# Cross attention in a decoder layer: the distance bias added by TensorE, maxima and exponentials taken for four tiles at once

## The chip, the core and the metric

The kernel runs on one core of a Trainium2 chip. The core has five engines that work side by side and each through its own list of instructions: TensorE (PE) multiplies matrices and writes its results to PSUM, VectorE (DVE) does elementwise work and reductions, ScalarE (ACT) does exponentials, other functions and copies, GpSimd (POOL) helps, and SyncE (SP) starts transfers. They wait for one another by semaphores. The metric is device time in microseconds (us). All data are fp32.

## The reference

One post-norm decoder layer for 4 batches of 1024 tokens of width 256: self attention with two further attentions nested in it, cross attention to 154 context tokens, and a mixture of experts. Each of the three parts is added to its input and normalised. The change concerns the cross attention, which has 16 heads of width 16:

```python
q = (query @ Wq.T + bq) * d ** (-0.5)
k = key_ @ Wk.T + bk
v = value @ Wv.T + bv
...
scores = jnp.einsum('bhqd,bhkd->bhqk', q, k)
distance_bias = -jnp.log(distances + 1e-09) * jnp.abs(distance_scaling)
scores = scores + distance_bias[:, None, :, :]
attn = jax.nn.softmax(scores, axis=-1)
out = jnp.einsum('bhqk,bhkd->bhqd', attn, v)
```

The bias depends on the batch, the query token and the context token, but not on the head: every head adds the same 1024 x 154 numbers.

## The kernel before, in words

The program goes through the batches one after the other and, at the end, through the experts for all of them. In a batch come the self attention, two attentions with four heads, a projection with a normalisation (close_sublayer), the cross attention, and a second such closing.

The cross attention first makes the keys kx, the values vx and the bias tile. The bias tile has the 128 tokens of a tile on its partitions and, for each of the 8 token tiles, 154 context tokens in a row; ACT takes the logarithm (line 942) and DVE the scaling (line 943). Then the loop of lines 951 to 961 runs over 32 units. Unit n belongs to a group g of four heads, a pair of token tiles tp, and a pair of heads in the group:

- scores(n), lines 654 to 689: four products on PE (line 662), one for each of 2 token tiles x 2 heads. Each takes 32 rows of q and of kx, so it uses 32 rows of PE's array; the two heads lie in different rows. The results, 4 x 154 columns, go to one PSUM tile called big, of which there are two for the whole kernel; each head has a bank of it. The helper biased (line 267) then lets DVE do a fused operation for each of the four: it adds bias, negates, stores the sum to the tile xs in SBUF and leaves its minimum in a column of xmx. ACT takes the exponential of each of the four with that column as its bias (line 682).
- flip(n), lines 691 to 706, two rounds later: eight transposes on PE (line 697) into two PSUM tiles called one, of which there are three, and copies back to SBUF, by ACT, or by DVE for the second half of odd units.
- product(n), lines 708 to 725, after each second unit: eight products on PE (line 716, sixteen records) weigh the values, a copy on ACT (line 724), and two rounds later, by the due times of the class Clock, divide (lines 351 to 355) transposes the result on PE and divides it by the row sums on DVE.

The softmax's sums come from a column of ones in the values, so nothing else is taken from the exponentials. The queries of the next four heads are projected at each eighth unit (lines 647 to 652 and 955), and the first ones before the loop.

In the first three batches the loop also takes one step a round of begin(b + 1), the generator that starts the next batch's self attention (maxima, which use big too, and value projections). In the last batch there is nothing to take. The framework orders each engine's instructions when the program is built, near program order, but it may draw work of this kind into a wait: in the first three batches PE does value projections (line 302) between the query projection and the first scores.

Of the kernel before, what the change touches and what calls it, by code (L numbers as in the profile page):

```python
# [8 lines left out]
F32 = mybir.dt.float32  # L9
I32 = mybir.dt.int32  # L10
U32 = mybir.dt.uint32
AF = mybir.ActivationFunctionType
ALU = mybir.AluOpType
AX = mybir.AxisListType
PSUM = bass.MemoryType.PSUM

P = 128
B, S, H = 4, 1024, 256
S2 = 154
# [27 lines left out]
def decoder_layer(ctx: ExitStack, tc: tile.TileContext, a, out):  # L47
    nc = tc.nc
# [8 lines left out]
    def big():  # L57
        return pbig.tile([P, 2, 512], F32, tag="big", name="big")

    def small():  # L60
        return pone.tile([P, 512], F32, tag="one", name="one")
# [18 lines left out]
    ident = const.tile([P, P], F32, name="ident")  # L80
# [52 lines left out]
    with tc.tile_pool(name="wA", bufs=1) as wA, tc.tile_pool(name="work", bufs=2) as work:  # L133
# [76 lines left out]
        ps = small()  # L210
# [53 lines left out]
        def ex_tile(shape, name):  # L264
            return work.tile(shape, F32, tag="ex", name=name, bufs=EXB)

        def biased(out, ps, bias, low):

            nc.vector.tensor_tensor_reduce(  # L269
                out=out,  # L270
                in0=ps,
                in1=bias,
                scale=-1.0,
                scalar=3.0e38,
                op0=ALU.add,
                op1=ALU.min,
                accum_out=low,
            )
# [239 lines left out]
        def mha_units(qk, v, weight, cx):  # L518
# [93 lines left out]
            for u in range(n + 2):  # L612
                pss = scores(u) if u < n else None
                if 1 <= u <= n:
                    flip(u - 1, 0)
                if u < n:
                    exponentials(u, pss)
                if 1 <= u <= n:
                    flip(u - 1, 1)
                    del probs[u - 1]  # L620
                if u >= 2:
                    product(u - 2)
                yield

        def out_features(w, cx, c):

            ps = big()
            for tb in range(2):
                for pair in range(2):
                    nc.tensor.matmul(  # L630
                        ps[:, tb, :],
                        w[4][:, pair, c * P : (c + 1) * P],
                        cx[:, pair, tb * 512 : (tb + 1) * 512],
                        start=(pair == 0),
                        stop=(pair == 1),
                    )
            return ps


        class Cross:  # L640
# [13 lines left out]
            def scores(self, n):  # L654
                g, s = divmod(n, 8)
                tp, pair = divmod(s, 2)
                ps = big()
                for tt in range(2):
                    for jj in range(2):
                        r = 32 * (2 * pair + jj)  # L660
                        tok = (2 * tp + tt) * P
                        nc.tensor.matmul(  # L662
                            ps[:, jj, tt * S2 : (tt + 1) * S2],
                            self.q[g][r : r + 32, tok : tok + P],
                            self.kx[r : r + 32, g, :],
                            start=True,
                            stop=True,
                        )
                ex = ex_tile([P, 2, 2, S2], "xs")
                mx = work.tile([P, 4], F32, tag="xmx", name="xmx", bufs=3)  # L670
                for tt in range(2):
                    for jj in range(2):
                        biased(
                            ex[:, jj, tt, :],
                            ps[:, jj, tt * S2 : (tt + 1) * S2],
                            self.bias[:, 2 * tp + tt, :],
                            mx[:, 2 * tt + jj : 2 * tt + jj + 1],
                        )
                for tt in range(2):
                    for jj in range(2):  # L680
                        i = 2 * tt + jj
                        nc.scalar.activation(  # L682
                            ex[:, jj, tt, :],
                            ex[:, jj, tt, :],
                            AF.Exp,
                            bias=mx[:, i : i + 1],
                            scale=-1.0,
                        )
                self.ex[n] = ex

            def flip(self, n):
# [120 lines left out]
        for b in range(B):  # L812
            y = ys[b]

            bias = work.tile([P, NT, S2], F32, tag="bias", name="bias", bufs=1)
# [39 lines left out]
            for c in range(NC2):  # L855
                ps = out_features(ca, cx2, c)
# [23 lines left out]
            for c in range(NC2):  # L880
                ps = out_features(mc, cx3, c)
# [14 lines left out]
            ps = big()  # L896
# [9 lines left out]
            ps = big()  # L906
            for g in range(NG):
                for c in range(NC2):
# [4 lines left out]
                        start=(c == 0),  # L913
                        stop=(c == NC2 - 1),
                    )
            for g in range(NG):
# [4 lines left out]
                    bias=xbk[:, g : g + 1],  # L921
# [3 lines left out]
            for k in range(2):  # L925
                ps = small()
                for c in range(NC2):
# [4 lines left out]
                        start=(c == 0),  # L932
                        stop=(c == NC2 - 1),
# [117 lines left out]
    ps = small()  # L1051
# [287 lines left out]
```

## Time and profile before

| what | value |
|---|---|
| median of 3 runs | 3434.65 us (3431.64 to 3437.42) |
| the profiled execution's own time | 3433.82 us |
| its span, first to last instruction | 3432.0 us |
| mean granted clock of TensorE | 0.976 |
| stretch 632 to 760 us, the first cross attention: PE / DVE / ACT busy | 125.09 / 75.75 / 80.96 of 128 us |
| stretch 2668 to 2776 us, the last one: PE / DVE / ACT busy | 101.24 / 63.37 / 75.01 of 108 us |
| flips of the cross attention, PE line 697 | 1024 records, mean 283 ns |
| scores of the cross attention, PE line 662 | 1024 records, mean 324 ns |

PE is the engine of matrix products, PEld its weight loads. A record's duration runs from its start to its modelled end, and records overlap: the share of time that PE advances is read from the distance between records, or from the chain of work that ended last, not from their mean. An fp32 product makes two records, a transpose one. The granted clock is 1.00 when TensorE gets its full clock.

### The profile page before, as it was taken

Reading aid. Unit: us, or ns where it says so; the run is one execution under the profiler, and the core shown is the slowest. Engines: PE = TensorE matmul, PEld = TensorE weight load, DVE = VectorE, ACT = ScalarE, POOL = GpSimd, SP = SyncE. Lnnn points to the kernel's source line nnn. Section 1 sums busy time; section 2 is a strip of 40 time slices with the busy share of each in tenths; the row PEclk is TensorE's granted clock in tenths of the full one; section 3 lists DMA queues with packets and bytes.
Section 4 is the critical chain, followed back from the end, with each engine's and each line's share of the span. In section 5 each row is a group of like instructions: output and inputs, shape, how many; then the busy total and the mean of one; then the engine's idle time right before and its main releaser. Section 6 shows DMA issues by size and latency. Waiting matters only on the chain.

```text
span 3432.0 us, 60936 instructions
## 1 busy us (share of the span) xinstructions
PE 3300.5 (96%) x25260; PEld 2085.6 (61%) x25260; DVE 1725.3 (50%) x3571; ACT 1601.0 (47%) x3130; POOL 373.3 (11%) x601
## 2 busy tenths in 40 slices
PE   7999999999999999999999999999999999999997
PEld 4555667565556675665566756555667665555554
DVE  3565555565655555656555556565556551122224
ACT  1555534375555453755554537555534731222223
POOL 4000000000000000000000000000000018222123
PEclk7999999999999999999999999999999999999999
DMA  9000000000000000000000000000000052111114
GB/s 204 1 2 1 1 1 1 3 21 14 1 1 1 1 1 3 21 13 2 1 1 1 1 3 9 1 2 1 1 1 1 1 203 82 47 42 44 44 44 157
DMA packets 75866, 84.13 MB, mean 25 GB/s; under 512 B 15136, under 2 KB 65928, under 8 KB 75592
## 3 DMA queue, kind: packets, MB, share of 16 engines
q1 hardware_dynamic: 68040, 61.53, 6.4%
q0 software_dynamic: 7552, 18.70, 1.6%
q8 instruction: 202, 3.31, 0.4%
q14 instruction: 72, 0.59, 0.1%
HBM read 46.52 MB, written 33.69 MB: 23 GB/s over the span
## 4 chain that ended last, share of the span: by engine, by line
PE 85%; DVE 9%; ACT 2%; issue 2%; POOL 1%; DMA 1%; SPq 0%; ACTq 0%; DVEq 0%; POOLq 0%
PE big L288 10%; PE big L422 8%; PE big L530 8%; PE one L566 7%; PE acc L584 7%; PE big L1226 7%; PE one L480 7%; DVE mxp L429 6%; PE one L460 4%; PE acc L1248 4%; PE one L697 3%; PE big L1178 3%; PE big L662 3%; PE one L302 2%; PE acc L716 2%
## 5 line engine op out<-in xcount | busy, mean ns | idle before, releaser
L429 DVE TENSOR_REDUCE mxp<-big 128x2 f32<-128x1024 f32 x512 | 610.3, 1218 | 305.5 <-PE acc L460 252.1
L422 PE MATMUL big<-k,q 31*128 31x512 f32 x2048 | 595.8, 644 | 30.2 <-DVE mxp L429 26.6
L471 ACT ACTIVATE ex<-one 128x512 f32<-128x512 f32 x696 | 391.3, 601 | 247.4 <-PE acc L460 182.9
L460 PE MATMUL one<-q,k 32*128 32x256 f32 x2784 | 501.9, 397 | 0.0
L269 DVE CUSTOM_DVE_ANT_0 prob<-big,zero_t 128x1024 f32<-128x1024 f32 x256 | 303.6, 1222 | 271.9 <-PE big L530 271.7
L460 PEld LDWEIGHTS one<-q,k 32*128 32x128 f32 x2784 | 326.8, 186 | 31.0 <-ACT ex L471 2.5
L549 ACT ACTIVATE prob<-prob,nmx 128x1024 f32<-128x1024 f32 x256 | 293.0, 1153 | 20.2 <-DVE nmx L269 19.7
L530 PE MATMUL big<-mk,mq 64*128 64x512 f32 x1024 | 284.4, 633 | 2.5 <-ACT ex L468 2.5
L422 PEld LDWEIGHTS big<-k,q 31*128 31x128 f32 x2048 | 180.1, 189 | 171.5 <-DVE mxp L429 93.6
L571 ACT COPY pt<-one 128x512 f32<-128x512 f32 x256 | 137.8, 588 | 311.7 <-PE one L566 311.7
L566 PEld LDWEIGHTS one<-ident,prob 128*128 128x128 f32 x2048 | 221.8, 142 | 98.1 <-issue 92.4
L1226 PE MATMUL big<-wall,xt 128*128 x576 | 272.5, 596 | 1.8 <-POOL by L1202 1.8
L460 PE MATMUL acc<-q,k 32*128 32x256 f32 x928 | 263.9, 404 | 0.0
L566 PE MATMUL one<-ident,prob 128*128 128x128 f32 x2048 | 257.6, 279 | 0.0
L480 PE MATMUL one<-ex,v 128*32 128x256 f32 x4096 | 248.4, 382 | 0.0
L1236 DVE TENSOR_TENSOR hidr<-big,slr 128x512 f32<-128x512 f32 x72 | 49.8, 691 | 332.7 <-ACT slr L1234 332.7
L682 ACT ACTIVATE xs<-xs,xmx 128x154 f32<-128x154 f32 x512 | 174.4, 414 | 69.6 <-DVE xmx L269 69.6
L480 PEld LDWEIGHTS one<-ex,v 128*32 128x32 f32 x4096 | 119.8, 110 | 122.1 <-ACT ex L471 35.8
L573 DVE COPY pt<-one 128x512 f32<-128x512 f32 x256 | 164.3, 683 | 10.9 <-PE one L566 10.9
L269 DVE CUSTOM_DVE_ANT_0 xs<-big,bias 128x154 f32<-128x154 f32 x512 | 132.0, 314 | 66.0 <-ACT avx L724 33.5
L530 PEld LDWEIGHTS big<-mk,mq 64*128 64x128 f32 x1024 | 99.6, 191 | 101.7 <-issue 79.4
L460 PEld LDWEIGHTS acc<-q,k 32*128 32x128 f32 x928 | 155.4, 186 | 0.0
(266 smaller groups left out, 4715.2 us busy)
## 6 DMA issues: line engine op xcount, KB each, us to landing
xg<-scratch SPq DMA_DIRECT2D x72, 129.0 KB, 2.0
scratch<-empty SPq DMA_DIRECT2D x1, 9216.0 KB
r<-result SPq DMA_DIRECT2D x8, 1024.0 KB, 11.2
y<-in_x_dram SPq DMA_DIRECT2D x4, 1024.0 KB, 5.3
wall<-in_L_ffn_w_gate_dram SPq DMA_DIRECT2D x8, 512.0 KB, 10.3
wall<-in_L_ffn_w_up_dram SPq DMA_DIRECT2D x8, 512.0 KB, 10.8
wall<-in_L_ffn_w_down_dram SPq DMA_DIRECT2D x8, 512.0 KB, 11.6
bias<-in_fside_BxSxS_dram SPq DMA_DIRECT2D x4, 616.0 KB, 4.5
```

What stands on the lines that cost most here:

```text
L269: nc.vector.tensor_tensor_reduce(out=out, in0=ps, in1=bias, scale=-1.0, scalar=3.0e38, op0=ALU.add, op1=ALU.min, accum_out=low,)
L288: nc.tensor.matmul(ps[:, tb, :], w[:, c, lo : lo + P], xT[:, c, tb * 512 : (tb + 1) * 512], start=(c == 0), stop=(c == NC2 - 1),)
L422: nc.tensor.matmul(ps[:, jj, :], st["q"][r : r + MR, tok : tok + P], st["k"][r : r + MR, kb * 512 : (kb + 1) * 512], start=True, stop=True,)
L429: nc.vector.reduce_max(mxp[:, t, kb, 2 * pair : 2 * pair + 2], ps, axis=AX.X)
L460: nc.tensor.matmul(scs[jj][:, i * QW : (i + 1) * QW], st["k"][r : r + MR + 1, kc * P : (kc + 1) * P], st["q"][r : r + MR + 1, part * QW : ...
L471: nc.scalar.activation(ex[:, jj, :], scs[jj], AF.Exp, scale=1.0 / HD**0.5)
L480: nc.tensor.matmul(av[32 * j : 32 * j + 32, 0:QW], self.v[:, kc, h * VW : h * VW + 32], exs[kc // 2, j // 2][:, j % 2, i : i + QW], start= ...
L530: nc.tensor.matmul(pss[i][:, kb, :], q[r : r + MD, t * P : (t + 1) * P], k[r : r + MD, kb * 512 : (kb + 1) * 512], start=True, stop=True,)
L549: nc.scalar.activation(p, p, AF.Exp, bias=nmx[:, i : i + 1], scale=-1.0, accum_out=sm[:, t % 4, i : i + 1],)
L566: nc.tensor.transpose(ps[:, kc * P : (kc + 1) * P], probs[u][i][:, at : at + P], ident)
L584: nc.tensor.matmul(av[64 * i : 64 * i + 64, (t % 4) * P : (t % 4 + 1) * P], v[:, kc, h * MD : (h + 1) * MD], flipped[u][i][:, kc, :], star ...
L1226: nc.tensor.matmul(ps[:, g, :], xt[:, c * P : (c + 1) * P], wall[:, bass.ds(off + (g * NC2 + c) * D, D)], start=(c == 0), stop=(c == NC2 - 1),
```

## The change

In scores, two products on PE now come first: the identity matrix ident, which the kernel has for its transposes, is the stationary operand and two token tiles of the bias, 308 columns, are the moving one. Each writes the bias to one bank of the PSUM tile, and the four score products add to what stands there. DVE takes the maximum over each of the four rows of 154 with one instruction (xmx is now 128 x 2 x 2) and subtracts the maxima from the scores with a second one that reads them spread over the row and writes xs. ACT takes one exponential over all 616 columns, with no bias and no scale. What is computed is the same: the exponential of the biased score less its row's maximum. Nothing else is changed.

```diff
                 ps = big()
+                for jj in range(2):
+                    nc.tensor.matmul(
+                        ps[:, jj, 0 : 2 * S2],
+                        ident,
+                        self.bias[:, 2 * tp : 2 * tp + 2, :].rearrange("p t k -> p (t k)"),
+                        start=True,
+                        stop=False,
+                    )
                 for tt in range(2):
                     for jj in range(2):
                         r = 32 * (2 * pair + jj)
...
                             self.kx[r : r + 32, g, :],
-                            start=True,
-                            stop=True,
+                            start=False,
+                            stop=(tt == 1),
                         )
+                sc = ps[:, :, 0 : 2 * S2].rearrange("p j (t k) -> p j t k", t=2)
+                mx = work.tile([P, 2, 2], F32, tag="xmx", name="xmx", bufs=3)
+                nc.vector.reduce_max(mx, sc, axis=AX.X)
                 ex = ex_tile([P, 2, 2, S2], "xs")
-                mx = work.tile([P, 4], F32, tag="xmx", name="xmx", bufs=3)
-                for tt in range(2):
-                    for jj in range(2):
-                        biased(
-                            ex[:, jj, tt, :],
-                            ps[:, jj, tt * S2 : (tt + 1) * S2],
-                            self.bias[:, 2 * tp + tt, :],
-                            mx[:, 2 * tt + jj : 2 * tt + jj + 1],
-                        )
-                for tt in range(2):
-                    for jj in range(2):
-                        i = 2 * tt + jj
-                        nc.scalar.activation(
-                            ex[:, jj, tt, :],
-                            ex[:, jj, tt, :],
-                            AF.Exp,
-                            bias=mx[:, i : i + 1],
-                            scale=-1.0,
-                        )
+                nc.vector.tensor_tensor(
+                    ex, sc, mx.unsqueeze(3).to_broadcast([P, 2, 2, S2]), ALU.subtract
+                )
+                nc.scalar.activation(ex, ex, AF.Exp)
                 self.ex[n] = ex
```

## The prediction

> **What bounds the kernel now.** I read the page's totals and its chain first:
>
> ```profile
> span 3432.0 us, 60936 instructions
> PE 3300.5 (96%) x25260; PEld 2085.6 (61%) x25260; DVE 1725.3 (50%) x3571; ACT 1601.0 (47%) x3130; POOL 373.3 (11%) x601
> PE 85%; DVE 9%; ACT 2%; issue 2%; POOL 1%; DMA 1%; SPq 0%; ACTq 0%; DVEq 0%; POOLq 0%
> ```
>
> TensorE carries 85% of the chain. But these are averages, and the change touches only the cross-attention loop (lines 951 to 961), which runs four times, 32 units each: by the instructions on tile xs 2670 to 2760 us in the last batch, and from 632, 1320 and 2006 us in the others. So next: busy time by stretches, in the last batch, where no work of a next batch is mixed in (columns: length, then PE, PEld, DVE, ACT, POOL busy, clock, DMA).
>
> ```profile
> 2710.00:2720.00 10.00, 10.00 (x110) 7.39 (x108) 6.40 (x38) 9.05 (x26) 0.00 (x0) 1.00 0.01 2
> 2730.00:2740.00 10.00, 10.00 (x108) 7.28 (x106) 6.75 (x40) 9.05 (x27) 0.00 (x0) 1.00 0.01 2
> ```
>
> PE never stops; but ACT is at 90%, so which of the two sets the pace? The chain, in order of time, through two units (start, length):
>
> ```profile
> 2712.76 1.09 PE one L697 x8
> 2713.86 1.00 PE acc L716 x16
> 2714.86 0.72 PE big L662 x8
> 2715.58 1.03 PE one L697 x8
> 2716.61 0.22 PE one L351 x2
> 2716.83 0.72 PE big L662 x8
> 2717.55 1.10 PE one L697 x8
> ```
>
> From 2712.76 to 2717.55 the pieces add to 4.79 us and all are PE: two score groups, two flips, one product, one division. ACT and DVE appear nowhere, so PE sets the pace and the others follow, ACT closely. Their work (count | busy, mean ns):
>
> ```profile
> L682 ACT ACTIVATE xs<-xs,xmx 128x154 f32<-128x154 f32 x512 | 174.4, 414 | 69.6 <-DVE xmx L269 69.6
> L269 DVE CUSTOM_DVE_ANT_0 xs<-big,bias 128x154 f32<-128x154 f32 x512 | 132.0, 314 | 66.0 <-ACT avx L724 33.5 <-PE big L662 29.3 <-ACT xs L682 2.6
> L429 DVE TENSOR_REDUCE mxp<-big 128x2 f32<-128x1024 f32 x512 | 610.3, 1218 | 305.5 <-PE acc L460 252.1 <-PE big L422 29.2 <-PE one L460 18.3
> L735 DVE TENSOR_TENSOR y<-one,y 128x512 f32<-128x512 f32 x32 | 22.0, 688 | 48.7 <-PE one L887 27.7 <-PE one L783 21.0
> ```
>
> Last, the loop's entry in the last batch, and what full-array fp32 products cost (the chain again):
>
> ```profile
> 2668.00:2672.00 4.00, 1.51 (x25) 1.16 (x24) 3.02 (x16) 1.32 (x2) 0.00 (x0) 1.00 0.01 2
> 2672.00:2676.00 4.00, 3.71 (x21) 2.63 (x18) 1.40 (x13) 4.00 (x13) 0.00 (x0) 0.72 0.00 0
> 2676.00:2680.00 4.00, 4.00 (x5) 1.47 (x5) 0.88 (x8) 2.05 (x6) 0.00 (x0) 0.50 0.00 0
> ```
>
> ```profile
> 2722.34 3.63 PE big L288 x8
> 2820.10 13.81 PE one L1155 x64
> 2835.88 27.79 PE big L1178 x64
> ```
>
> PE idles 2.5 us at the entry, then the granted clock falls to half.
>
> [...]256 columns take 13.81/64 = 0.216 us a record, 512 take 27.79/64 = 0.434[...]. [...]The trace shows half clock after each entry to the loop, although PE had paused only 1.4 to 2.5 us in 4.[...]
>
> **PE, the path.** Added per unit: two products of the 128x128 identity with 308 bias columns, in fp32. A product makes two records (L1178: 256 records, 128 products), so four records. 308 columns x 27.79/64/512 us = 0.261; from the 256-column row, 308 x 0.843 ns = 0.260. I take 0.26: 4 x 0.26 = 1.04 us. [...]Their weight loads (0.19 us each for 128x128, L1178) fit under 0.26 of streaming, except the first: L288 behind a score group takes 3.63 us for eight records that stream in 8 x 0.43 = 3.44, so 0.19 is exposed. Behind a flip it may be hidden. The trace has no identity product here; bounds 0 and 0.2, and I take 0.1. Below nothing is possible too, if the score group's own first loads now hide under the identity's streaming; that I keep for a rival. Sum 1.14 us x 128 units = 146 us. The four score products stay as they are; adding to what stands in PSUM is the same streaming.
>
> **DVE.** Removed: four fused add-minimums, which follow one another every 0.24 us and end with a 0.08 us read-out (0.24 x 3 + 0.32 + 0.08 = 1.1 us). Added: a maximum over 616 elements, [...]0.79 us[...], and a subtraction, 0.80. So about +0.5 us a unit, +64 in all. Hidden: the stretch shows DVE at 6.4 of 10 us, that is 3.1 of 4.79 per two units; it becomes 4.1 of 4.79 + 2 x 1.14 = 7.07. With no cover it would cost those 64 us.
>
> **ACT.** Removed: four exponentials of 154, 1.36 us in a row by the timeline. Added: one of 616, between 512 (601 ns, L471) and 1024 (1153, L549): 0.75. Saves 0.6 a unit, 77 in all, worth nothing: PE is in front. No DMA or queue order changes.
>
> **Waits.** The first product now waits for the bias tile (Ln on ACT, scaling on DVE, lines 942 and 943), which is done before the transposes of y and the query projection; nothing. Behind a score group in DVE's queue stand the odd units' flip copy and the division; they start 0.5 us later. The big buffer is freed 1.75 us after the scores (0.16 until DVE sees them, 0.79, 0.80) and not 1.2; with two buffers it is wanted one flip (1.06) and one full score group (1.76) later. The exponential ends 2.5 us after the scores, where the four ended after 1.9 to 2.1 (ACT could start on the first piece); the flip two units later finds it ready all the same, and the copies behind it end at about 3.5; the next flip starts at 2.9 to 3.9. That margin is thin: about nothing on average, a rival below.
>
> **Entry.** In the last batch PE waits 1.38 us for the queries (DVE, 1.28), 1.11 for a buffer and 0.3 for the first exponentials. The identity products of unit 0 need no queries and go into the first gap; the second is filled by the longer unit 1. I leave 0.7 of 2.8: -2.1 us. In the other batches PE idles 1.44 there, and value projections already fill the wait for queries; a longer maximum and subtraction eat what the products fill: 0. By the clock column in stretches of 4 us, the half clock lasts 13.7, 10.2, 10.2 and 6.9 us after the four entries, so it costs half of 41, 20.5 us. I assume that it goes in the last batch (-3.4) and is one window of 3.4 shorter in the others (-1.7 each): -8.5; bounds 0 and -20.5.
>
> **Sum.** 146 - 2.1 - 8.5 = +135. On the profiled execution: span 3432.0 + 135 = 3567; that execution took 3433.8 with 1.8 around the span, 0.8 under the median. Predicted median 3434.65 + 135 = 3570.
>
> **Rivals.**
> 1. *PE absorbs part.* The score group's eight records take 0.72 us, but stream only 8 x 154 x 0.84 ns / 2 (two row groups at once) = 0.52. If their loads hide under the identity's streaming, 0.2 x 128 = 26 us come back, the exposed load (13) is none and the half clock all goes (12 more): +84, 3519. For: PEld is idle 27% there.[...]
> 2. *A new wait takes over.* The late subtraction delays exponential, copies and the small buffers (three for five uses in two units), and PE stands. At 0.3 us a unit: 38 us, +173, 3608. For: the margin of 0.4 or less above. Against: every step is shorter than PE's 3.5 us a unit.
> 3. *Not slower.* ACT, not PE, sets the present pace (90%; the flip's weights start 0.15 us after an ACT copy), and the identity products run in PE slack. Then DVE's 4.1 us sets two units in place of 4.79: -44 us, 3391. The kernel is not slower only if a unit's products cost PE under 10.6/128 = 0.08 us, the entry's gains; from there this rival decides. Against: the records are back to back, and 308 columns on all rows can't be had for nothing.
> 4. *The change doesn't do what it says:* the identity products could run in one record each as the transposes do (L697: one record per transpose): 67 us less, +68, 3503. Against: they are no transposes, and every fp32 product in the page makes two records.
>
> **How the numbers follow.** Forecast 0.62 (own range 3545 to 3595: exposed load 0 to 0.2, which is 13 us either way, and the clock's -20 to 0). Rival 1 0.13, rival 2 0.17, rival 3 0.04, rival 4 0.04. Measured change under 0.2% (7 us) could not be told from none. Range 3512 to 3612: it reaches past the centres of rivals 1 and 2 and leaves out rivals 3 and 4 (0.08), nearly half of rival 2 (0.08) and the lower end of rival 1 (0.03). Slower holds all but rival 3: 0.96; faster 0.03, same 0.01.
>
> **What would show it.** Right: in the last batch's loop PE stays at 10.00, two units take about 7.07 us in the chain, identity records 512 last about 0.26 back to back, DVE at 0.79 and 0.80, ACT falls to some 45%. Wrong: PE idle before scores or flips for DVE or ACT (rival 2); score groups under 0.72 (rival 1); 256 records (rival 4). The largest risk is the size per unit: the exposed load and the clock at the entry.

## The result, and the profile after

The changed kernel takes 3552.68 us (median of 4 runs, 3551.47 to 3553.61) against 3433.35 before (median of 4 runs; the table further up has 3 of them): 1.0345 times as long, 95% interval 1.0333 to 1.0357, or +119 us. The prediction said 3570, +135, in a range of 3512 to 3612. The profiled execution's span went from 3432.0 to 3550.3 us, +118.3.

The page of the changed kernel, its totals and its chain by engine:

```profile
span 3550.3 us, 60846 instructions
PE 3421.5 (96%) x25772; PEld 2157.8 (61%) x25772; DVE 1796.4 (51%) x2803; ACT 1534.8 (43%) x2746; POOL 372.6 (10%) x601
PE 82%; DVE 9%; POOL 3%; issue 2%; DMA 2%; ACT 2%; SPq 0%; ACTq 0%; DVEq 0%; POOLq 0%
```

PE has 121 us more to do, and the span is 118 us longer. DVE has 71 us more and ACT 66 less; the time follows PE. The last batch's loop by stretches, as it was shown of before (length, then PE, PEld, DVE, ACT and POOL busy, clock, DMA):

```profile
2810.00:2820.00 10.00, 10.00 (x93) 6.75 (x91) 6.13 (x12) 4.61 (x8) 0.00 (x0) 1.00 0.01 2
2840.00:2850.00 10.00, 10.00 (x83) 7.10 (x81) 6.20 (x12) 5.09 (x9) 0.00 (x0) 1.00 0.01 2
```

PE is still at 10.00; ACT fell from 9.05 to between 4.6 and 5.1. The chain in order of time through two units:

```profile
2801.29 1.03 PE one L693 x8
2802.32 0.22 PE one L351 x2
2802.54 1.04 PE big L659 x4
2803.58 0.72 PE big L670 x8
2804.30 1.03 PE one L693 x8
2805.33 1.00 PE acc L712 x16
2806.33 1.23 PE big L659 x4
2807.57 0.72 PE big L670 x8
```

From 2801.29 to 2808.29 a pair of units takes 7.00 us (4.79 before; forecast 7.07). All pieces but the two on L659, the identity products, are there as before. They take 1.04 us behind a division and 1.23 us behind a product. The groups that the change made (count | busy, mean ns | idle before):

```profile
L659 PE MATMUL big<-bias,ident 128*128 128x308 f32 x512 | 158.9, 433 | 5.0 <-DVE xs L681 5.0
L679 DVE TENSOR_REDUCE xmx<-big 128x4 f32<-128x616 f32 x128 | 102.4, 800 | 149.8 <-PE big L670 149.8
L684 ACT ACTIVATE xs<-xs 128x616 f32<-128x616 f32 x128 | 91.7, 717 | 67.7 <-DVE xs L681 66.8
```

There are 512 identity records, two a product. PE waited 5.0 us for the subtraction in the whole program, and all the idle time ahead of DVE's new maximum was a wait for PE: PE leads.

At the entry to the loop the picture changed more than forecast. The first batch by stretches of 4 us, before:

```profile
632.00:636.00 4.00, 2.56 (x24) 1.31 (x22) 3.77 (x19) 2.43 (x5) 0.00 (x0) 1.00 0.00 0
636.00:640.00 4.00, 4.00 (x16) 2.36 (x17) 1.59 (x6) 1.47 (x5) 0.00 (x0) 0.50 0.00 0
640.00:644.00 4.00, 4.00 (x12) 2.01 (x11) 1.85 (x9) 2.31 (x6) 0.00 (x0) 0.50 0.00 0
```

and after:

```profile
632.00:636.00 4.00, 3.17 (x21) 1.73 (x20) 3.47 (x5) 0.27 (x1) 0.64 (x1) 1.00 0.00 0
636.00:640.00 4.00, 3.16 (x20) 1.64 (x20) 2.90 (x4) 2.22 (x3) 0.00 (x0) 1.00 0.00 0
640.00:644.00 4.00, 4.00 (x26) 2.41 (x25) 2.78 (x5) 1.92 (x4) 0.00 (x0) 1.00 0.00 0
```

PE still stands, twice for 0.83 us or a little more, for the subtraction that frees the big buffer, but none of these stretches has more than 0.84 us of idle time, where one had 1.44; the clock stays at 1.00. So it is at all four entries. That the shorter pauses are the reason is not shown by this; the section on the clock below comes back to it.

### The profile page after: what moved, and what is told of

It is laid out like the page before. It is cut to its first block, busy times and chain, and to the rows that moved or that the text cites. A ratio compares the mean times of both kernels' runs of the same rounds, so it can differ in the third digit from the quotient of the medians.

```text
span 3550.3 us, 60846 instructions
## 1 busy us (share of the span) xinstructions
PE 3421.5 (96%) x25772; PEld 2157.8 (61%) x25772; DVE 1796.4 (51%) x2803; ACT 1534.8 (43%) x2746; POOL 372.6 (10%) x601
## 4 chain that ended last, share of the span: by engine, by line
PE 82%; DVE 9%; POOL 3%; issue 2%; DMA 2%; ACT 2%; SPq 0%; ACTq 0%; DVEq 0%; POOLq 0%
PE big L288 9%; PE big L530 7%; PE big L422 7%; PE one L566 7%; PE acc L584 7%; PE one L480 7%; PE big L1222 7%; DVE mxp L429 6%; PE one L460 4%; PE big L659 4%; PE acc L1244 4%; PE one L693 3%; PE big L670 3%; PE one L302 2%; PE acc L712 2%
## 5 line engine op out<-in xcount | busy, mean ns | idle before, releaser
L429 DVE TENSOR_REDUCE mxp<-big 128x2 f32<-128x1024 f32 x512 | 610.3, 1218 | 298.7 <-PE acc L460 250.7
L701 ACT COPY xpt<-one 77x512 f32<-77x512 f32 x192 | 105.4, 582 | 227.5 <-PE one L693 227.4
L679 DVE TENSOR_REDUCE xmx<-big 128x4 f32<-128x616 f32 x128 | 102.4, 800 | 149.8 <-PE big L670 149.8
L659 PE MATMUL big<-bias,ident 128*128 128x308 f32 x512 | 158.9, 433 | 5.0 <-DVE xs L681 5.0
```

The lines of the kernel that those rows point to most:

```text
L429: nc.vector.reduce_max(mxp[:, t, kb, 2 * pair : 2 * pair + 2], ps, axis=AX.X)
L659: nc.tensor.matmul(ps[:, jj, 0 : 2 * S2], ident, self.bias[:, 2 * tp : 2 * tp + 2, :].rearrange("p t k -> p (t k)"), start=True, stop=False,)
```

## Experiments

Theory A: PE sets the pace, the identity products are the whole cost, and the same products close the gaps at the entry to the loop and so keep PE's clock up. Theory B: the relief of DVE and ACT keeps the clock up. Rivals from the prediction: ACT set the pace before; part of the products hides; a new wait takes over.

Two sums from each trace serve to compare. "Loops" is the time from the first query projection of a batch to the first transpose of its result (line 370), over four batches. "Half clock" is the time at clock 0.50 that began within the first 20 us or so of a loop, over four batches. Both are of the one execution of each kernel that was profiled; the medians are of 4 to 21 executions. In the kernel before, from 2676 to 2682 us, records of 512 columns (L288) start 0.853 us apart at clock 0.50 and 0.430 us apart at 1.00, so half of the time at half clock is taken as lost.

| kernel | median us | ratio, 95% interval | loops us | half clock us |
|---|---|---|---|---|
| before | 3433.35 | | 458.4 | 41.0 |
| after | 3552.68 | 1.0345 (1.0333 to 1.0357) | 569.7 | 0 |
| e1, no identity products | 3458.69 | 1.0071 (1.0058 to 1.0085) | 456.4 | 54.6 |
| e1b, the same, last unit as before | 3437.72 | 1.0007 (1.0001 to 1.0014) | 457.7 | 51.2 |
| e2, identity products alone | 3556.01 | 1.0359 (1.0343 to 1.0375) | 571.0 | 0 |
| e3, first three units changed | 3432.18 | 0.9996 (0.9988 to 1.0004) | 450.5 | 0 |
| e4, all but the first three changed | 3557.53 | 1.0363 (1.0347 to 1.0379) | 570.0 | 23.9 |
| e5, identity products twice | 3686.60 | 1.0738 (1.0723 to 1.0754) | 701.0 | 0 |
| e6, first unit changed | 3438.76 | 1.0012 (1.0004 to 1.0020) | 461.6 | 30.7 |
| e7, product ahead of flip | 3536.58 | 1.0302 (1.0287 to 1.0317) | 560.3 | 0 |
| e8, before with an early table load | 3422.10 | 0.9969 (0.9957 to 0.9981) | 438.6 | 0 |
| e9, e3 with an early table load | 3431.26 | 0.9991 (0.9982 to 0.9999) | 451.5 | 0 |

The ratios are to runs of the kernel before on the same chip (medians 3432.4 to 3434.0). Where the intervals of two ratios overlap, the difference between these two kernels is not clear of noise.

### The DVE and ACT part alone

e1 takes the identity products out of the changed kernel:

```diff
                 ps = big()
-                for jj in range(2):
-                    nc.tensor.matmul(
...
-                    )
...
-                            start=False,
-                            stop=(tt == 1),
+                            start=True,
+                            stop=True,
```

> The changed kernel without the identity products: DVE's one maximum and one subtraction and ACT's one exponential stay, the distance bias is left out of the computation. Theory A (PE sets the pace; the identity products are the whole cost, and they are also what keeps PE's clock up at the entry to the loop): PE has the work of before, so the time is that of before, 3428 to 3436 us, a pair of units takes 4.7 to 4.8 us, and the half clock after the four entries is back, some 41 us of it. Theory B (what keeps the clock up is the relief of DVE and ACT at the entry): the half clock stays away, 3410 to 3418 us. Rival (ACT set the pace before): a pair takes about 4.1 us and the time is under 3400 us.

It took 25 us more than the kernel before, which neither theory allows. But the loops took 456.4 us, 2 less than before: the time was lost elsewhere. The waits of ACT in the first 120 us of the program:

```profile
ACT bias L930 <- DMA bias<-in_fside_BxSxS_dram: 64.7, 3, 51.0
```

Without a reader of the bias tile, the order made at build had drawn the logarithms of all four batches to the start of ACT's list, where they waited up to 51 us for a transfer. The first loop began at 647.7 us and not at 627.2. That is a fault of the experiment, so e1b keeps a reader: unit 31 of each batch goes the way of before.

```diff
+                if n < 31:
+                    self.scores_pe(n)
+                else:
+                    self.scores_dve(n)
```

(scores_pe is scores of e1 here, scores_dve that of the kernel before.)

> As the run without identity products (the distance bias left out), but the last unit of each batch goes the way of before and still reads the bias tile, so that the logarithms of later batches can't be drawn to the start of the program, where they held up ACT for the transfer of the bias. Theory A (PE sets the pace, and the 21 us lost before the first cross attention were those logarithms): the loops take 455 to 458 us in all and the time is 3428 to 3438 us. Rival (the maximum and the subtraction by themselves make the kernel slower, through DVE): 3450 to 3460 us again.

With 3437.72 us and loops of 457.7 it is the kernel before within a few us, and its first loop begins at 628.1 us again. The loop without identity products (chain of e1b):

```profile
2716.76 0.72 PE big L668 x8
2717.48 1.03 PE one L728 x8
2718.51 0.22 PE one L351 x2
2718.72 0.72 PE big L668 x8
2719.45 1.03 PE one L728 x8
2720.48 1.00 PE acc L747 x16
```

A pair takes 4.72 us. ACT's exponentials are shorter and DVE's work is longer, and the pace stays PE's: the rival that ACT set the pace (4.1 us a pair) is out. So is theory B: with the relief and no identity products the half clock is there, and longer, 51.2 us.

### The PE part alone

e2 adds the products to the kernel before and leaves DVE and ACT as they were, so the bias counts twice.

```diff
                 ps = big()
+                for jj in range(2):
+                    nc.tensor.matmul(
+                        ps[:, jj, 0 : 2 * S2],
+                        ident,
+                        self.bias[:, 2 * tp : 2 * tp + 2, :].rearrange("p t k -> p (t k)"),
+                        start=True,
+                        stop=False,
+                    )
...
-                            start=True,
-                            stop=True,
+                            start=False,
+                            stop=(tt == 1),
```

> The kernel before with the identity products added and nothing else; DVE still adds the bias, so that the bias counts twice. Theory A: as the changed kernel, 3550 to 3557 us, a pair of units takes 7.0 us, and no half clock at the four entries. Theory B: the half clock is there as before, 3570 to 3577 us.

It took 3556.01 us and has no half clock at the entries, as theory A says. That is 3.3 us more than the changed kernel, and the intervals of the two ratios overlap (1.0343 to 1.0375 and 1.0333 to 1.0357): the whole DVE and ACT part of the change is worth a few us at most, and none for certain.

### The price of a product

e5 makes each identity product twice.

```diff
-                for jj in range(2):
+                for jj, again in ((0, 0), (0, 1), (1, 0), (1, 1)):
...
-                        start=True,
+                        start=(again == 0),
```

> The changed kernel with each identity product made twice (the bias counts twice). Theory A: four more records of 0.26 us a unit and no further exposed load, 128 x 1.03 = 132 us more than the changed kernel, 3680 to 3690 us; two units take 9.1 us. Rival (part of each product hides in waits of PE): clearly less than 132 us more; or, if PE was not alone on the path, more.

134 us more than the changed kernel, and 131.3 more in the loops: 131.3/128/4 = 0.256 us a record. Its chain shows that nothing but the four records is added behind a product and behind a division:

```profile
2901.65 2.27 PE big L659 x8
2905.89 2.08 PE big L659 x8
```

against 1.23 and 1.04. The 0.19 us behind the product stays one.

### The exposed load

e7 puts product ahead of flip in each round, so that no identity product follows value products.

```diff
-                if 2 <= n < total + 2:
-                    xa.flip(n - 2)
                 if n >= 4 and n % 2 == 1:
                     xa.product(n - 4)
+                if 2 <= n < total + 2:
+                    xa.flip(n - 2)
```

> The changed kernel with product ahead of flip in each round, so that an identity product always follows a flip or a division, never a product. The theory that 0.19 us of weight load stands exposed where the identity follows the value products: 64 times 0.19 = 12 us less than the changed kernel, 3538 to 3543 us, and all identity groups take 1.04 us in the chain. Rival (the 0.19 us are paid wherever full-array work follows value products): the flip behind the product pays them, 3550 to 3555 us.

It took 16 us less than the changed kernel, a little below the forecast of 3538 to 3543. Its chain:

```profile
2787.04 1.03 PE one L693 x8
2788.07 0.22 PE one L351 x2
2788.29 1.04 PE big L659 x4
2789.32 0.72 PE big L670 x8
2790.05 1.00 PE acc L712 x16
2791.05 1.03 PE one L693 x8
2792.08 1.04 PE big L659 x4
2793.12 0.72 PE big L670 x8
```

Both identity groups take 1.04 us, and the flip behind the product 1.03 as ever: the 0.19 us belonged to the 128-column load (0.190 us in the mean, PEld on L659 of the changed kernel) behind value products that use 32 columns each, and the transposes don't pay it. (Their own loads have 77 columns, so whether a transpose with 128 would pay it is open.) A pair takes 6.80 us, 64 x 0.20 = 13 us; the loops show 9.4, and the 3 to 4 us between are not accounted for. The rest of the 16 lies outside the loops, where this execution's half clock is 13.7 us shorter in all (6.9 us of time).

### What keeps the clock up

e3 mixes the two ways in one loop, as in the diff; e4 has n >= 3 in its place, and e6 n < 1.

```diff
+                if n < 3:
+                    self.scores_pe(n)
+                else:
+                    self.scores_dve(n)
```

> The changed way in the first three units of each batch, the way of before in the other 29. Theory A: the clock stays up at the entries (20.5 us less) and 12 units pay 1.1 us each (13 us), so 3422 to 3430 us. If the clock needs the identity products all through the loop: the half clock comes a few us later, 3440 to 3448 us. Theory B as theory A, since the first units have the relief too.

> The way of before in the first three units of each batch, the changed way in the other 29. Theory A and B: the half clock after the entries is back, at least 20 to 41 us of it, and 116 units pay 1.1 us each: 3433 + 128 less what a shorter half clock gives, 3551 to 3562 us. If the clock stays up by what comes later in the loop: 3540 to 3543 us.

> The changed way in the first unit of each batch only. Theory A (a denser entry keeps the clock up): 4 units pay 1.1 us or less, and if one unit's products are enough the half clock stays away at the entries: 3416 to 3424 us. If the clock needs more than one unit: the half clock comes as before, 3432 to 3438 us.

e4 has twelve units without identity products, worth 12 x 1.1 = 13 us, and yet it is no faster than the changed kernel (3557.53 against 3552.68 us): without the products in the first three units, 23.9 us of half clock come back. So it is the first units' products that count, not those later in the loop. e3 shows the other side in its profiled execution: no half clock, loops 7.9 us shorter, as forecast (13 - 20.5). Its median missed the forecast of 3422 to 3430 and is no shorter than before: its executions lie between 3425.8 and 3437.4 us, at mean clocks from 0.982 to 0.978, so in the longer ones the clock was lower somewhere. Whether at the entries or elsewhere, the one trace can't show. e6, with products in one unit, has 30.7 us of half clock, but its profiled execution (3445.14 us) is one of the slowest of 21, which go from 3424.27 us at a mean clock of 0.980 to 3445.86 at 0.974. One unit's products are not enough in every execution; whether they are in some, no trace shows. The median, 3438.76 us, is just above the forecast for a half clock as before.

Is it then the length of PE's pauses that decides? The clock records of the traces before and after change only on a grid of 3.41 us: every stretch between two changes is a whole multiple of it, and so are the half-clock sums of the table. One such period of the kernel before, ahead of its second fall at an entry, and one of the changed kernel, from the first entry:

```profile
1322.12:1325.53 3.41, 2.83 (x21) 1.77 (x23) 2.18 (x10) 3.20 (x9) 0.00 (x0) 1.00 0.00 0
638.48:641.89 3.41, 2.57 (x17) 1.58 (x16) 2.65 (x5) 0.72 (x1) 0.00 (x0) 1.00 0.00 0
```

PE idles 0.58 us in the first, and the clock is 0.50 in the period after it; it idles 0.84 us in the second, and the clock stays up. Elsewhere in the changed kernel's trace the clock fell behind a period in which PE had records all the time, most of them products of 8 columns:

```profile
818.28 3.74 PE L791 MATMUL one<-gw,x2T 128*128 128x8 f32 x32
819.39:822.80 3.41, 3.41 (x36) 3.19 (x38) 0.88 (x4) 0.15 (x1) 0.00 (x0) 1.00 0.73 252
822.80:826.22 3.42, 3.42 (x23) 2.26 (x16) 2.13 (x4) 1.68 (x4) 0.00 (x0) 0.50 0.00 0
```

So idle time alone does not decide. In the period of the kernel before PE starts 16 records of score products, which use 31 or 32 rows, and 3 transposes; in that of the changed kernel it starts 8 of these, 3 transposes and four identity records, 308 columns each on all rows. Whether that difference decides, no run tests by itself.

In the kernel before, the last thing that PE waits for at the entry is the first exponentials, and ahead of these ACT loads a table for 1.28 us, after the first minimum has come. e8 takes one column's exponential earlier, so that the load comes under the query projection:

```diff
             xa = Cross(x1T, kx, vx, bias, xtok)
+            warm = work.tile([P, 1], F32, tag="warm", name="warm", bufs=2)
+            nc.scalar.activation(warm, x1T[:, 1, S - 1 : S], AF.Exp)
             xa.project_q(0)
```

> The kernel before with one more instruction a batch: ACT takes an exponential of one column of x1T ahead of the first query projection, so that its table load (1.28 us) runs under the projection and not between the first maxima and the first exponentials. If the load stands on the path at the four entries: 1.3 us less at each, 5 us in all, 3427 to 3429 us; if the shorter gap also keeps PE's clock up: up to 20 us more, 3408 to 3415 us. If the wait for the big buffer covers the load: no change, 3431 to 3435 us.

> The changed way in the first three units of each batch and the early table load. If PE stands at the entry for DVE's subtraction (buffer) only: as the run with the first three units alone, 3427 to 3435 us. If the load was on the path there as well and what was left of the gaps made the clock fall in some executions: 3418 to 3424 us, with less scatter between executions.

ACT at the last entry, by the timeline (start, length), first of the kernel before and then of e8:

```profile
2670.67 1.28 ACT L682 ACT_TABLE_LOAD   x1 [5.52 <-DVE xmx L269]
2671.96 3.87 ACT L682 ACTIVATE xs<-xs,xmx 128x154 f32<-128x154 f32 x12
2651.94 1.28 ACT L950 ACT_TABLE_LOAD   x1
2653.24 0.20 ACT L950 ACTIVATE warm<-x1T 128x1 f32<-128x1 f32 x1
2657.40 3.88 ACT L682 ACTIVATE xs<-xs,xmx 128x154 f32<-128x154 f32 x12 [3.96 <-DVE xmx L269]
```

In e8 the exponentials start at once when DVE's first minimum is there. In its profiled execution PE idles 0.94 us at the first three entries in place of 1.44, the loops are 19.8 us shorter than before, and there is no half clock at any entry. Half of the 41.0 us of before is 20.5, so the clock is the whole gain, and the load's own 1.28 us a batch are not to be seen in it. The kernel takes 0.9969 times as long (0.9957 to 0.9981), 12 us less: with nothing of the change in it, it has the lowest median of the study. That median, 3422.10 us, lies between the forecasts: the profiled execution is the fastest of six (3414.69 us, mean clock 0.981), and the slowest (3427.88, 0.977) is near the forecast without the clock. So the gain of the clock isn't had in full each time, and where the slower ones lose it is not shown. e8 also says that identity products are one way to keep the clock up, not the only one. e9 adds the early load to e3 and gains nothing clear on e3, as forecast for an entry where PE stands for the subtraction.

## Why the prediction was right, and where it was off

**What bounds the kernel.** Right. PE set the pace at 4.79 us a pair and sets it at 7.00; e1b excludes ACT, and e2 shows that the rest of the change is worth a few us at most.

**The identity products, 146 us.** Right in size. The chain has 35.7, 35.7, 35.7 and 35.1 us of them in the four loops, 142 together, or 1.11 a unit where 1.14 was taken. The record was put at 0.26 us and streams in 0.256 (e5); in the loop of the changed kernel the identity records start one at a time, 0.26 us apart, and the 32-row score records two at a time, 0.13 us from pair to pair. The exposed load was put at 0.1 between 0 and 0.2: it is 0.19 behind a product and nothing behind a flip or a division, and e7 confirms the place. The middle came out right because half of the units follow a product; the prediction hadn't named that place, so there is some luck in it. The score groups take 0.72 us before and after, so adding to what stands in PSUM cost nothing here, as assumed.

**DVE and ACT.** 0.79 and 0.80 us were forecast, 0.800 and 0.799 measured; ACT 0.75 and 0.717. The two for DVE were my estimates. For the subtraction the trace of before leads to the same: elementwise operations of 128, 256 and 512 elements take 291, 419 and 688 ns (L355, L346, L735), by which I estimate 688 + 104 x 1.034 = 796 ns for 616. For the maximum of 616 it had one size alone to go by, 1024 in 1218 ns (L429). Hidden, as said.

**Waits.** Right for the steady loop: no pause of PE. At the entry of the first three batches the subtraction holds PE twice for 0.83 us, 1.7 us in place of 1.44, about what the old waits cost, as said. In the last batch 0.34 us of idle time is left of 2.8 before; 0.7 was forecast.

**The clock at the entry, -8.5 us.** This is the mis-sized term. It was given bounds of 0 and -20.5, and I took the half clock as gone in the last batch and 3.4 us shorter in the others, an assumption by the steps in which the half clocks of before differ (13.7, 10.2, 10.2 and 6.9 us). It was gone at all four entries: -20.5. That is 12 of the 17 us by which the sum was too high against the span. The step that failed was to let the clock follow PE's summed idle time at the entry: in the first three batches that time did not fall (1.44 us before, 1.7 after), and the half clock went all the same. The products in the first three units are what keeps it away (e3, e4); by what, beyond the shape of the pauses, stays open.

**The rest.** 142 - 20.5 would give +122 in the loops; they grew by 111.3. On the chain of the first loop ACT and DVE pieces fell from 15.8 to 9.8 us, which fits that PE fills more of the loop's waiting than forecast; no run takes it apart. Outside the loops the span grew by 7.0 us, 3.4 of them from a longer half clock right after the first loop. Neither was forecast, and that they nearly cancel is luck.

**Rivals.** Rival 1 needed score groups under 0.72 us: they are at 0.72 in the steady loop, and only its clock part came. Rival 2 needed PE to stand in the loop: it does only at the entry. Rivals 3 and 4 are out by e1b and by the 512 records.

## What to carry to other kernels

Before work is moved from one engine to another, ask which of them the chain names: here 71 us more on DVE and 66 less on ACT were worth a few us at most, and 1.1 us more on PE was paid 128 times. Price a product by the columns that stream (here a record took 0.216 us for 256 columns, 0.256 for 308 and 0.434 for 512), and look at what stands before it for the load that is exposed (here 0.19 us behind the value products). Look also at the clock behind a few us in which PE pauses or has only small products: in the kernel before up to 13.7 us at half clock followed 1.44 us of pauses at an entry, and in the changed kernel 3.4 us followed 3.74 us of products of 8 columns. A table load moved out of such a place gave more than any part of the change, 12 us by the median.

## What the runs showed of the hardware that was not expected

- PE's clock at the entry: before, half clock of 10.2 to 13.7 us followed 1.44 us of idle time in the first three batches; after, 1.7 us at the same entries were followed by none. PE idled 0.58 us in the 3.41 us ahead of a fall in the kernel before, and 0.84 us in a period that no fall followed in the changed one. What decides it, no run shows.
- Of the identity products' weight loads in the steady loop, only the first behind value products that use 32 columns each was exposed, for 0.19 us; behind a flip or a division it was hidden (1.23 against 1.04 us, e7).
- Logarithms at the head of ACT's list that waited for a transfer, up to 51.0 us, put off the first loop by some 20 us (e1: 647.7 us against 627.2): instructions with no reader were not free here.
